# A conditioned residual block with paged attention: condition weights selected on chip, second tile transposed by TensorE, three transfers moved to other places in their queues

## The chip, the cores and the metric

The kernel runs on one core of a Trainium2 chip. The core has TensorE (PE, matmuls; PEld is its weight load), VectorE (DVE), ScalarE (ACT), GpSimd (POOL) and the sync engine (SP), which here only issues DMAs. The metric is the device time of one launch in microseconds (us). Times are given as the median of several runs; one further execution was recorded by the profiler and is what all rows are taken from.

## The reference

The input x has 64 sequences (B) of 32 tokens (S) with 512 features (HID), float32. Two layers are added to it in turn.

```python
# layer 0: every sequence has a condition 0..15; its 32x32 matrix mixes the tokens
x = x + einsum('bct,bcd->bdt', x, weights[condition])
# layer 1: attention over a paged cache, 32 query heads, 8 key heads, D = 128
q, k, v = x @ Wq.T, x @ Wk.T, x @ Wv.T          # 4096, 1024, 1024 wide
q, k = rope(rmsnorm(q) * q_norm_w, pos), rope(rmsnorm(k) * k_norm_w, pos)
# cached keys and values: 16 pages of 32 rows per sequence, by block table
scores = q @ concat(k_cache[table], k).T / sqrt(128), cached rows >= cache_seqlens masked
x = x + softmax(scores) @ concat(v_cache[table], v) @ Wo.T
```

`pos` is the sequence's cache length plus the token's number. The block table and the lengths are inputs, so pages are addressed from registers or by indirect DMA.

## The kernel before

**Tiles and steps.** A tile is 4 sequences x 32 tokens = 128 rows, so there are 16 tiles (NT). The heads are done in two halves (hh = 0, 1) of 4 key heads and 16 query heads; a step is one tile of one half, 32 steps in all. The second half reads back what the first left in DRAM: the partial output `acc_d` (`x1_a`, L344) and the transposed mixed input `x1t_d` (`x1_t`, L350).

**A step.** The tile's input is mixed by a block-diagonal 128x128 matrix `bd`, which holds four condition matrices (`x1_c`, L356: one matmul, one addition on DVE), and transposed by PE (`x1_b`, L363; ACT copies it to `x1t` and stores it). Then come projections of 512 columns each, four accumulating matmuls: one for k, one for v and four for q (`project`, L401). k and q pass through `norm_rope` (L409): a square on ACT, a mean and five passes on DVE, a power on POOL. Their result has tokens in the partitions and has to be turned, so that the head dimension lies there. In the first tile PE does that (`to_columns`, L483: four transposes per projection, two copies by ACT). In all other tiles DVE transposes blocks of 32x32 into `rows` (`turn_rows`, L451), and 16 DMAs of 80 KB from SP move the blocks across partitions into `q_cols` (batches 0 to 2) and `q_last` (batch 3) (`spread`, L463). `by_tensor` (L473) chooses.

**A batch** is one sequence of a step. SP loads its 16 key pages of 64 KB (`load_k`, L280; two buffers `k_t`, so the pages of the batch after next wait until the present one's keys are copied out), DVE copies each head's keys to `kh` (`head_keys`), PE computes the scores of the cached keys (`ps`), ACT their exponential (`pr`), PE the values (`po`), DVE the normalisation. Cached values come by indirect DMA from POOL (`fetch`, L311, rows in `v_row`), and ACT masks them into place (`fill`, L328). The new tokens' scores are made once per step (`new_scores`, `psn`, L584) and their values after that (`new_values`, `pnv`, L601). The output projection of the step before stands in slots 8 and 9 (`pout`, L512).

**Order.** A step has 16 slots (4 batches x 4 key heads). The loop from L909 writes the order out by hand, slot by slot; `pieces` (L866) says which parts of the next tile's preparation go into which slot. PE and SP execute in exactly that order (`manual_schedule`, L88); DVE, ACT and POOL do so in the opening, and are ordered by the scheduler after it. Each engine and each DMA queue runs in order, so one that waits holds up all that stands behind it.

**The opening** (L765 to L864) is written by hand for the first tile and part of the second. SP issues the input and the first query weight, then the 16 pages of the first batch, then the query weight 2, the value weight, the second tile's input, the query weight 3. POOL gathers the first tile's condition matrices row by row (`w_sel`, L771, by an index made on DVE in L726), then issues the key weight, query weight 1, and the page table and lengths for all batches (`pages_at`, `lens_at`). From those DVE makes `v_row` and the masks (`cached_rows`, L160). Filler matmuls (`keep_warm`, L787) run on PE in between. The second tile's k and v projections stand in the opening, its q projections in slots 4 to 7.

**Weights of the second half** are brought in parts near the change of halves: those of k, q, v by SP in steps 14 and 15, the eight parts of the output weights (each two DMAs of 256 KB) by POOL in steps 16 and 17 (`second_outputs`, L908).

Of the kernel before, what the change touches and what calls it, by code (L numbers as in the profile page):

```python
# [11 lines left out]
F32 = mybir.dt.float32  # L12
I32 = mybir.dt.int32
AF = mybir.ActivationFunctionType
ALU = mybir.AluOpType
AX = mybir.AxisListType
# [33 lines left out]
WARM = 16  # L50
# [5 lines left out]
def cond_resid_paged_attention_kernel(  # L56
# [130 lines left out]
    def steps_of(exact, pools):  # L187
# [46 lines left out]
        def load_w(kind, hh, g=0, part=slice(0, 4), eng=nc.sync):  # L234
# [11 lines left out]
            if kind == "o" and not exact:  # L246
                src = src.rearrange("(h j p) e -> h p j e", h=REP, p=S)
                for h in range(part.start, part.stop):
                    eng.dma_start(t[h * S : (h + 1) * S, :, :], src[h])
                return  # L250
            eng.dma_start(t[:, part, :], src.rearrange("(c p) e -> p c e", p=P)[:, part, :])

        def load_parts(which, hh, at, eng=nc.sync):

            if 0 <= at < 2 * len(which):
                kind, g = which[at // 2]
                load_w(kind, hh, g, slice(at % 2 * 2, at % 2 * 2 + 2), eng)
# [22 lines left out]
        def load_k(hh, b):  # L280
# [12 lines left out]
            for j in range(NPP):  # L293
# [12 lines left out]
            last_k[:] = [ins.ins]  # L306
            return k_raw
# [165 lines left out]
        def by_tensor(st):  # L473
            return st.n == 0 or exact
# [8 lines left out]
        def to_columns(st, i):  # L483

            pt = transposed(rows[:, :, i, :], f"{i}_{st.name}")
            p4 = pt.rearrange("p h (b s) -> p b h s", b=BT)
            n = BT - 1
            nc.scalar.copy(q_cols[:, :, i, :].rearrange("p b (h s) -> p b h s", h=4), p4[:, 0:n])  # L488
            nc.scalar.copy(
                columns(st, n)[:, i, :].rearrange("p (h s) -> p h s", h=4), p4[:, n]  # L490
            )
# [48 lines left out]
        class Batch:  # L540


            def __init__(self, st, bt):
                self.st, self.bt = st, bt
                self.n = st.n * BT + bt
                self.name = f"{st.name}_{bt}"
                self.b = st.t * BT + bt
                self.k_raw = load_k(st.hh, self.b)
                self.k, self.pr = {}, {}
                self.v_t = v_bufs[self.b % 2]  # L550
# [173 lines left out]
        if not exact:  # L724
            nc.scalar.dma_start(cond_0, cond[:, 0:1])
            nc.vector.tensor_scalar(cond_0, cond_0, float(S), row, ALU.mult, ALU.add)  # L726
# [3 lines left out]
        if exact:  # L730
# [34 lines left out]
        first, second = steps[0:2]  # L765
        x1_a(first)
        load_w("q", 0, 0)
        nc.scalar.dma_start(lens_sb, lens)
        nc.scalar.dma_start(freq, inv_freq.partition_broadcast(P))
        w_sel = work.tile([P, S], F32, tag="o", name="w_sel", bufs=1)  # L770
        nc.gpsimd.indirect_dma_start(  # L771
            out=w_sel,
            out_offset=None,
            in_=w_cond,
            in_offset=bass.IndirectOffsetOnAxis(ap=cond_0, axis=0),
        )
        nc.scalar.dma_start(cond_row, cond.rearrange("(i s) t -> s t i", s=S)[0:1])
        load_w("k", 0, eng=nc.gpsimd)
        load_w("q", 0, 1, eng=nc.gpsimd)
        batch = Batch(first, 0)  # L780
        load_w("q", 0, 2)
# [3 lines left out]
        later = Batch(first, 1)  # L785

# [10 lines left out]
        positions()  # L797
        trig = work.tile([P, 3, TRIG * HD], F32, tag="w1", name="trig0", bufs=1)
        angles(0, trig)
# [3 lines left out]
        x1_c(first)  # L803
        keep_warm(6)
# [46 lines left out]
        v_a(second)  # L851
# [14 lines left out]
        def pieces(st):  # L866
            do = {
# [10 lines left out]
            if st is second:  # L878
                do[2] = do[3] = do[13] = ()
            return do  # L880
# [27 lines left out]
        second_outputs = [(0, 10), (0, 13), (0, 15), (1, 1), (1, 3), (1, 4), (1, 5), (1, 6)]  # L908
        for st in steps:  # L909
# [3 lines left out]
            for bt in range(0 if st.n else 1, BT):  # L913
                this, after = batch, None
                n = st.n * BT + bt + 2
                if n < NHH * NT * BT:
                    after = Batch(steps[n // BT], n % BT)
                    unfilled += [(after, c) for c in range(VC)]
                for g in range(GH):
# [35 lines left out]
                    if slot == 13 and beyond:  # L955
                        x1_t(beyond)
# [8 lines left out]
                    if (st.n - NT, slot) in second_outputs:  # L965
                        at = second_outputs.index((st.n - NT, slot))
                        load_parts(outputs, 1, at, nc.gpsimd)
# [95 lines left out]
```

## Time and profile before

| what | us |
|---|---|
| median of 3 runs (lowest, highest) | 2183.66 (2181.93, 2184.26) |
| the profiled execution's own time | 2188.01 |
| its span, first to last instruction | 2186.2 |
| PE busy | 2150.5 |
| DVE busy | 1199.1 |
| ACT busy | 866.9 |
| POOL busy | 813.1 |

The granted clock of TensorE is 0.995 on average. In a row of the order in time, "x8" counts instructions that were merged into it, and the bracket gives the engine's idle time before it and what ended it. A float32 matmul is recorded as two instructions, so a projection of four is "x8".

### The profile page before, as it was taken

What the parts mean: (1) busy time and instruction counts of PE and PEld (TensorE: products, weight loads), DVE (VectorE), ACT (ScalarE), POOL (GpSimd) and SP (SyncE); (2) the same over time, 40 slices, a digit from 0 to 9 for tenths busy, and PEclk for the clock granted to TensorE, in tenths of its full rate; (3) what the DMA queues carried; (4) which work ended last, traced back from release to release, by engine and by line L of the source; (5) the groups of instructions that cost most, each with busy time, mean ns of one, the idle gap of its engine ahead of it and who ended that gap; (6) DMA issues with size and microseconds to landing.
All of it is one profiled execution on the core that took longest, in us unless ns stands there. A gap on an engine that the chain in (4) does not pass through costs nothing.

```text
span 2186.2 us, 41553 instructions
## 1 busy us (share of the span) xinstructions
PE 2150.5 (98%) x12970; PEld 1498.3 (69%) x12970; DVE 1199.1 (55%) x2881; ACT 866.9 (40%) x1574; POOL 813.1 (37%) x1024
## 2 busy tenths in 40 slices
PE   8889999999999999999999999999999999999998
PEld 5657776677766677766776667777667777667775
DVE  5655556665465554555554556545556445556442
ACT  3434444444333444333433334443334433334441
POOL 4433333343333433343334434333334333334330
PEclk9999999999999999999999999999999999999999
DMA  8665555556555555556767655555555555555651
GB/s 245 172 166 161 169 159 150 153 159 171 157 152 142 167 161 165 158 146 195 237 176 198 174 154 165 167 163 163 149 158 162 170 163 160 149 160 158 175 159 57
DMA packets 386839, 358.78 MB, mean 164 GB/s; under 512 B 54736, under 2 KB 316896, under 8 KB 386608
## 3 DMA queue, kind: packets, MB, share of 16 engines
q1 hardware_dynamic: 340608, 210.90, 34.3%
q0 software_dynamic: 42992, 140.86, 22.6%
q10 hardware_dynamic: 3008, 4.25, 0.5%
q8 instruction: 106, 1.74, 0.3%
q14 instruction: 125, 1.02, 0.2%
HBM read 302.59 MB, written 12.58 MB: 144 GB/s over the span
## 4 chain that ended last, share of the span: by engine, by line
PE 95%; DMA 2%; issue 1%; DVE 1%; ACT 0%; SPq 0%; POOL 0%; ACTq 0%; DVEq 0%; POOLq 0%
PE po_x L631 21%; PE ps_x L573 20%; PE pout_x L519 20%; PE pp_q_x L404 19%; PE pp_k_x L404 5%; PE pp_v_x L404 5%; PE pnv_x L615 2%; PE psn_x L591 1%; DMA raw_x<-in_vc_dram,v_row 1%; PE pmix_x L360 1%; DMA pages_at<-in_pages_v_dram 0%; DMA x1t_x<-x1t_d 0%; DMA k_t_x<-in_kt_dram 0%; PE px1t_x L368 0%; SPq L468 0%
## 5 line engine op out<-in xcount | busy, mean ns | idle before, releaser
L318 POOL DMA_INDIRECT raw_x<-in_vc_dram,v_row x512 | 538.2, 1051 | 828.3 <-ACT v_x L331 756.2
L581 ACT ACTIVATE pr_x<-ps_x 128x512 f32<-128x512 f32 x512 | 305.7, 597 | 818.2 <-PE ps_x L573 757.3
L631 PEld LDWEIGHTS po_x<-v_x,pr_x 128*128 128x128 f32 x4096 | 516.1, 192 | 129.8 <-issue 115.4
L631 PE MATMUL po_x<-v_x,pr_x 128*128 128x129 f32 x4096 | 551.6, 278 | 4.9 <-ACT v_x L331 1.9
L404 PE MATMUL pp_q_x<-wq_x,x1t_x 128*128 128x512 f32 x1024 | 462.5, 594 | 3.4 <-ACT kh_x L564 3.4
L519 PE MATMUL pout_x<-wo_x,ot_x 128*128 128x512 f32 x1024 | 450.2, 592 | 0.0
L573 PE MATMUL ps_x<-q_cols_x,kh_x 128*128 128x128 f32 x3072 | 405.7, 275 | 0.5 <-ACT q_cols_x L488 0.2
L573 PEld LDWEIGHTS ps_x<-q_cols_x,kh_x 128*128 128x128 f32 x3072 | 376.3, 192 | 17.1 <-issue 16.6
L331 ACT ACTIVATE v_x<-raw_x,valid 128x512 f32<-128x512 f32 x512 | 363.2, 716 | 16.5 <-DMA raw_x<-in_vc_dram,v_row 16.5
L519 PEld LDWEIGHTS pout_x<-wo_x,ot_x 128*128 128x128 f32 x1024 | 189.7, 190 | 214.3 <-issue 214.3
L404 PEld LDWEIGHTS pp_q_x<-wq_x,x1t_x 128*128 128x128 f32 x1024 | 185.4, 191 | 188.8 <-issue 185.2
L566 DVE COPY kh_x<-k_t_x 128x512 f32<-128x512 f32 x506 | 206.1, 417 | 191.8 <-PE ps_x L573 162.0
L649 DVE TENSOR_TENSOR nv_x<-po_x,nv_x 128x258 f32<-128x258 f32 x256 | 108.3, 423 | 317.7 <-PE po_x L631 282.5
L421 POOL TENSOR_TENSOR rs_q_x<-ms_q_x,minus_half 128x4 f32<-128x4 f32 x128 | 140.2, 1096 | 175.9 <-DVE ms_q_x L419 174.8
L414 ACT ACTIVATE sq_q_x<-pp_q_x 128x512 f32<-128x512 f32 x128 | 76.4, 597 | 271.9 <-PE pp_q_x L404 165.3
L573 PE MATMUL ps_x<-q_last_x,kh_x 128*128 128x128 f32 x1024 | 135.2, 275 | 2.9 <-DVE kh_x L566 2.9
L527 DVE TENSOR_TENSOR acc_x<-pout_x,acc_x 128x512 f32<-128x512 f32 x32 | 22.1, 692 | 199.5 <-PE pout_x L519 199.5
L573 PEld LDWEIGHTS ps_x<-q_last_x,kh_x 128*128 128x128 f32 x1024 | 124.6, 192 | 3.1 <-issue 3.1
L404 PE MATMUL pp_k_x<-wk_x,x1t_x 128*128 128x512 f32 x256 | 118.1, 605 | 2.8 <-DMA x1t_x<-x1t_d 2.5
L418 DVE TENSOR_REDUCE ms_q_x<-sq_q_x 128x4 f32<-128x512 f32 x128 | 86.4, 675 | 53.2 <-ACT sq_q_x L414 51.2
L404 PE MATMUL pp_v_x<-wv_x,x1t_x 128*128 128x512 f32 x256 | 115.2, 592 | 0.0
L652 DVE TENSOR_TENSOR o_x<-nv_x,rden 128x256 f32<-128x256 f32 x256 | 108.5, 424 | 6.5
(106 smaller groups left out, 1472.3 us busy)
## 6 DMA issues: line engine op xcount, KB each, us to landing
k_t_x<-in_kt_dram SPq DMA_DIRECT2D x2048, 64.0 KB
q_cols_x<-rows_x SPq DMA_DIRECT2D x372, 80.0 KB
q_last_x<-rows_x SPq DMA_DIRECT2D x124, 80.0 KB
raw_x<-in_vc_dram,v_row POOLq DMA_INDIRECT x512
acc_x<-in_x_dram SPq DMA_DIRECT2D x16, 256.0 KB
x1t_d<-x1t_x ACTq DMA_DIRECT2D x16, 256.0 KB
wo_x<-in_wo_dram SPq DMA_DIRECT2D x16, 256.0 KB
acc_d<-acc_x SPq DMA_DIRECT2D x16, 256.0 KB
```

The lines of the kernel that those rows point to most:

```text
L318: nc.gpsimd.indirect_dma_start(out=raw.rearrange("p g d -> p (g d)"), out_offset=None, in_=vc, in_offset=bass.IndirectOffsetOnAxis(ap=v_ro ...
L331: nc.scalar.activation(v_bufs[b % 2][:, c, :, 0:D], raw, AF.Copy, scale=ok)
L404: nc.tensor.matmul(pp, st.x1t[:, c, :], w[:, c, :], start=(c == 0), stop=(c == KC - 1))
L418: nc.vector.tensor_reduce(ms, sq, AX.X, ALU.add)
L421: nc.gpsimd.tensor_tensor(rs, ms, minus_half, ALU.pow)
L519: nc.tensor.matmul(st.po, st.ot[:, i, :], wt["o", st.hh, i // 4][:, i % 4, :], start=(i == 0), stop=(i == QH - 1),)
L566: last["dve"] = nc.vector.tensor_copy(k, ba.k_raw[:, :, g, :]).ins
L573: nc.tensor.matmul(ps[:, c, :], ba.k[g][:, c * P : (c + 1) * P], queries(ba, g), start=True, stop=True,)
L581: last["act"] = nc.scalar.activation(pr, ps, AF.Exp, scale=SCALE).ins
L631: nc.tensor.matmul(ba.po[:, g % 2, :], ba.pr[g][:, c, :], ba.v_t[:, c, g, :], start=(c == 0), stop=(c == VC - 1),)
L649: nc.vector.tensor_tensor(t, ba.po, t, ALU.add)
L652: nc.vector.tensor_tensor(ba.o[:, both, :], t[:, :, 0:D], rd.unsqueeze(2).to_broadcast([P, 2, D]), ALU.mult,)
```

## The change

- **Condition weights.** The gather and its index are gone. SP loads all 16 matrices (64 KB) into the first 32 partitions, right behind the first tile's input; three copies put them into the other partition groups; DVE compares each row's condition with the numbers 0 to 15 (from an iota on POOL), multiplies and sums, and fills `bd`. The mixing `x1_c(first)` now stands ahead of `positions` and the first `angles`. The first filler is 10 matmuls rather than 16.
- **Third query weight.** `load_w("q", 0, 2)` goes from SP, behind the first batch's pages, to POOL's queue, behind query weight 1 and ahead of `pages_at` and `lens_at`.
- **Second tile.** `by_tensor` holds for it too: no DVE transposes of blocks and no spread. `to_columns` takes the engine of its copies: ACT for k, DVE for the four q; they stand in slots 12 to 14 of the first step. `v_a(second)` moves from the opening to slot 13.
- **Input read back.** A step's last batch issues only the first eight of its sixteen pages; the others follow in slot 13, after `x1_t`.
- **Output weights of the second half.** SP issues them, and in other slots: part 0 in step 16, parts 1 to 7 in step 17.

```diff
-WARM = 16
+WARM = 10
...
             if kind == "o" and not exact:
                 src = src.rearrange("(h j p) e -> h p j e", h=REP, p=S)
                 for h in range(part.start, part.stop):
-                    eng.dma_start(t[h * S : (h + 1) * S, :, :], src[h])
+                    nc.sync.dma_start(t[h * S : (h + 1) * S, :, :], src[h])
...
-        def load_k(hh, b):
+        def load_k(hh, b, first_pages):
...
-            for j in range(NPP):
+            def load_page(j):
                 ins = nc.sync.dma_start(
...
-            last_k[:] = [ins.ins]
-            return k_raw
+                last_k[:] = [ins.ins]
+
+            for j in range(first_pages):
+                load_page(j)
+            return k_raw, [lambda j=j: load_page(j) for j in range(first_pages, NPP)]
...
         def by_tensor(st):
-            return st.n == 0 or exact
+            return st.n < 2 or exact
...
-        def to_columns(st, i):
+        def to_columns(st, i, copy=nc.scalar.copy):
...
-            nc.scalar.copy(q_cols[:, :, i, :].rearrange("p b (h s) -> p b h s", h=4), p4[:, 0:n])
-            nc.scalar.copy(
-                columns(st, n)[:, i, :].rearrange("p (h s) -> p h s", h=4), p4[:, n]
-            )
+            copy(q_cols[:, :, i, :].rearrange("p b (h s) -> p b h s", h=4), p4[:, 0:n])
+            copy(columns(st, n)[:, i, :].rearrange("p (h s) -> p h s", h=4), p4[:, n])
...
             nc.scalar.dma_start(cond_0, cond[:, 0:1])
-            nc.vector.tensor_scalar(cond_0, cond_0, float(S), row, ALU.mult, ALU.add)
...
+        number_i = small.tile([P, NCOND], I32, tag="number_i", name="number_i", bufs=1)
+        nc.gpsimd.iota(number_i, pattern=[[1, NCOND]], base=0, channel_multiplier=0)
         x1_a(first)
+        w_all = work.tile([P, NCOND, S], F32, tag="pr", name="w_all", bufs=3)
+        nc.sync.dma_start(w_all[0:S], w_cond.rearrange("(n s) e -> s n e", s=S))
         load_w("q", 0, 0)
...
-        w_sel = work.tile([P, S], F32, tag="o", name="w_sel", bufs=1)
-        nc.gpsimd.indirect_dma_start(
-            out=w_sel,
-            out_offset=None,
-            in_=w_cond,
-            in_offset=bass.IndirectOffsetOnAxis(ap=cond_0, axis=0),
-        )
...
         load_w("k", 0, eng=nc.gpsimd)
         load_w("q", 0, 1, eng=nc.gpsimd)
+        load_w("q", 0, 2, eng=nc.gpsimd)
         batch = Batch(first, 0)
-        load_w("q", 0, 2)
         load_w("v", 0)
...
-        positions()
-        trig = work.tile([P, 3, TRIG * HD], F32, tag="w1", name="trig0", bufs=1)
-        angles(0, trig)
+
+        for i, copy in enumerate((nc.vector.tensor_copy, nc.scalar.copy, nc.vector.tensor_copy), 1):
+            copy(w_all[i * S : (i + 1) * S], w_all[0:S])
+        own = small.tile([P, NCOND], F32, tag="own", name="own", bufs=1)
+        nc.vector.tensor_copy(cond_f, cond_0)
+        nc.vector.tensor_scalar(own, number, cond_f, None, ALU.is_equal)
+        nc.vector.tensor_tensor(
+            w_all, w_all, own.unsqueeze(2).to_broadcast([P, NCOND, S]), ALU.mult
+        )
+        w_sel = work.tile([P, S], F32, tag="o", name="w_sel", bufs=1)
+        nc.vector.tensor_reduce(w_sel, w_all.rearrange("p n e -> p e n"), AX.X, ALU.add)
         for i in range(BT):
             blk = slice(i * S, (i + 1) * S)
             nc.vector.tensor_copy(bd[blk, blk], w_sel[blk, :])
         x1_c(first)
+        positions()
+        trig = work.tile([P, 3, TRIG * HD], F32, tag="w1", name="trig0", bufs=1)
+        angles(0, trig)
         keep_warm(6)
...
-        v_a(second)
...
         def pieces(st):
...
+            if st is second:
+                by_vector = nc.vector.tensor_copy
+                return {
+                    4: (lambda st: q_a(st, 0),),
...
+                    12: (lambda st: to_columns(st, GH), lambda st: to_columns(st, 0, by_vector)),
+                    13: (v_a, lambda st: to_columns(st, 1, by_vector)),
+                    14: (
+                        lambda st: to_columns(st, 2, by_vector),
+                        lambda st: to_columns(st, 3, by_vector),
+                    ),
+                }
...
-        second_outputs = [(0, 10), (0, 13), (0, 15), (1, 1), (1, 3), (1, 4), (1, 5), (1, 6)]
+        second_outputs = {
+            (0, 10): (0,),
+            (1, 2): (1,),
+            (1, 4): (2,),
+            (1, 5): (3, 4),
+            (1, 6): (5, 6),
+            (1, 7): (7,),
+        }
...
-                    after = Batch(steps[n // BT], n % BT)
+                    after = Batch(steps[n // BT], n % BT, NPP // 2 if bt == BT - 1 else NPP)
...
-                    if slot == 13 and beyond:
-                        x1_t(beyond)
+                    if slot == 13:
+                        if beyond:
+                            x1_t(beyond)
+                        for load in after.pages_left if after else ():
+                            load()
...
-                        load_parts(outputs, 1, at, nc.gpsimd)
+                        load_parts(outputs, 1, at)
```

## The prediction

> **What bounds the kernel now.** I read the page's busy times first, then the waits of TensorE (PE), then the order in time around each wait.
>
> ```profile
> PE 2150.5 (98%) x12970; PEld 1498.3 (69%) x12970; DVE 1199.1 (55%) x2881; ACT 866.9 (40%) x1574; POOL 813.1 (37%) x1024
> ...
> PE psn_x L591 <- DMA q_cols_x<-rows_x: 7.7, 1, 7.7
> PE pp_q_x L404 <- ACT kh_x L564: 3.4, 1, 3.4
> PE ps_x L573 <- DVE kh_x L566: 2.9, 1, 2.9
> PE pp_k_x L404 <- DMA x1t_x<-x1t_d: 2.5, 1, 2.5
> PE po_x L631 <- ACT v_x L331: 1.9, 2, 1.3
> ```
>
> PE is busy 98% of the span, so only its waits (us in total, times, longest) and slow stretches can be shortened. By the order in time nearly all fall before 119 us; from there PE is busy throughout (the windows 120 to 1000 and 1500 to 2100 us show no idle time), but for one wait at 1066, one at 1198 and the tail. What the change can win lies in the opening and in those two. The lines that carry them (start us, us, engine line, what; in brackets the idle time before and its releaser):
>
> ```profile
> 7.01 8.96 DMA pages_at<-in_pages_v_dram
> ...
> 16.06 0.35 DVE L164 TENSOR_SCALAR v_row<-pages_at,row 128x256 int32<-128x256 int32 x1 [2.88 <-DMA pages_at<-in_pages_v_dram]
> ...
> 22.48 0.39 SPq L251 DMA_DIRECT2D wq_x<-in_wq_dram  x1
> ...
> 29.86 5.37 PE L404 MATMUL pp_q_x<-wq_x,x1t_x 128*128 128x512 f32 x8 [3.37 <-ACT kh_x L564]
> ...
> 94.62 0.70 DVE L454 STREAM_TRANSPOSE rows_x<-rope_q_x 128x512 f32<-128x512 f32 x1
> ...
> 97.23 6.51 SPq L468 DMA_DIRECT2D q_cols_x<-rows_x  x8
> 110.22 2.41 SPq L468 DMA_DIRECT2D q_last_x<-rows_x  x4
> ...
> 116.72 0.60 PE L591 MATMUL psn_x<-q_cols_x 128*32 128x128 f32 x2 [7.74 <-DMA q_cols_x<-rows_x]
> ...
> 1193.25 0.37 SPq L354 DMA_DIRECT2D x1t_x<-x1t_d  x1
> ...
> 1200.99 5.37 PE L404 MATMUL pp_k_x<-wk_x,x1t_x 128*128 128x512 f32 x8 [2.45 <-DMA x1t_x<-x1t_d]
> ```
>
> The reader is to see: PE stood at 26.5 for the third query weight, which SP issued at 22.48 behind 16 key pages (the ACT copy named as releaser was only the last other event); it stood 7.74 us for the second tile's spread, four of whose DMAs left SP at 110.22; and at 1198 for the projection input, issued behind a batch's 16 pages.
>
> **1. The condition weights (L771, L802).** Out goes a gather that POOL issues in 1.04 us; bd was complete at 10.20. In comes a 64 KB load right behind the input's on SP, three copies between partition groups (two on VectorE (DVE), one on ACT), a compare, a multiply, a reduce, and the same four copies to bd. The load's landing isn't in this trace. Bounds: not before the condition column (chain: 0.74 + 3.12 = 3.86), not after the weight issued behind it was in (about 7); I take 4.7, as it is nearer to the first in size. Then DVE: 2 x 0.42 (as kh copies 128x512), about 0.25 for the small two, 0.69 (as L361), 0.69 (as L418), 0.79 for bd: 3.3 us, bd at 8.0, 2.2 us sooner. PE adds 1.87 (pmix), DVE 0.69: mixed input at 10.6 instead of 12.85. But positions and the first angles now follow that addition on DVE: 0.4 + 2.1 us (7.09 to 9.16 before), then ACT's sine, abs and cosine (9.19 to 10.13 before: 0.94), and on ACT these stand ahead of the x1t copy (14.85 before). 10.6 + 0.4 + 2.1 + 0.94 gives 14.0: the copy gains 0.8 at best and loses 2.2 if the load lands at 7. Neither moves the end: what the first projections feed, DVE's chain from 16.06, waits for pages_at. Value: 0. WARM 16 to 10 only shortens filler in that wait.
>
> **2. Third query weight on POOL's queue (L782).** It is issued before pages_at and lens_at, which wait behind it on that queue. Its 1.05 MB at the 295 GB/s of the window 10 to 20 us take 3.6 us; on the other side POOL is free of the gather (1.04) and of its wait for the condition (1.04), so wk leaves 2.0 us sooner. pages_at lands S later: bounds 0 (the sooner start used in full and transfers closer packed) and 3.6 (start useless); I take 1.5. Behind pages_at stand, in DVE's order, the row numbers, four masks, the second angles and the norms of q0, k, q1, q2, each 3.6 us (21.51, 25.12, 28.74). The fourth started at 35.95, because its matmul ended at 35.23; freed of the weight it follows the third at 32.4 + S. ACT's squares, key copies and exponentials hang on that. Gain 3.55 - S = 2.1 (0 to 3.5). SP, one DMA lighter, issues wv at about 22.5, and wv is needed at 33.
>
> [...] The row: the DMA engines were 89% and 93% busy from 10 to 30 us. [...] I keep S = 1.5.
>
> **3. Second tile by TensorE, values projection in slot 13.** Removed: 16 spread DMAs on SP (0.59 each), five DVE transposes (0.71 each), the wait of 7.74 and the slow work after it: psn took 2.12 (1.01 in the next step), the po after it 1.60 (1.06): 1.65. Added on PE: 20 transposes, 0.44 per four (46.84 to 47.28): 2.2. Added copies: two on ACT (0.47, 0.28), eight on DVE, where PSUM reads of 128x258 take 0.43: some 2.8 us, at slots 12 to 14, with DVE idle 3.3 and 12 us just after. The last copies have 4.9 us of PE work ahead of new_scores to hide in (pmix 0.86, px1t 0.44, four groups of 0.9); without that cover they would cost about 1.5. Sure part: 7.74 + 1.65 - 2.2 = 7.2.
>
> v_a (3.44 us of PE at 52.98) leaves the opening for slot 13. The new_scores, fills, gathers and the query norms then start 3.4 us sooner, and DVE (busy 9.8 of 10 us at 80 to 90) loses 0.63 us net per query. Four PE waits in 74 to 102 hang on these: 0.59, 1.45, 2.90, 1.34, together 6.3. I take 4.0 back (0 to 6.3): PE gets to them sooner too, and gathers compete with wo loads (a gather issued at 65.74 landed at 74.0). Key pages of the following batches, freed from the spread on SP, aren't late.
>
> **4. Input read back sooner, outputs on SP.** With eight pages deferred, x1t's load leaves 8 x 0.54 = 4.3 us sooner and no output weights of POOL's queue contend. The two waits go: 2.45 and 0.39. Also pp_k at 1200.99 took 5.37 instead of 3.60: 1.77. [...] The row says 4.6: the granted clock was 0.68 in 1201 to 1206.4. (After the 2.90 us at 94.6 it stayed 1.00, so the wait's length doesn't settle it.) I take the row. Cost: 14 wo DMAs go to SP in step 17; 12 stand ahead of the third batch's pages and take 12 x 0.47 = 5.6, and SP was idle there from 1215.7 to 1225.2. Their 3 MB may delay gathers: 0.3 (0 to 1.5). Value 4.3. In the 14 steps without the wait nothing changes, nor in the first half of the steps, where the deferred pages follow the others at once.
>
> **Sum.** 0 + 2.1 + 7.2 + 4.0 + 4.3 = 17.6 us of the profiled span of 2186.2: 2168.6. That execution took 2188.01, 4.35 above the median shown; on the median 2183.66 - 17.6 = 2166.
>
> **Rivals.**
> *Waits re-form (0.24).* Part 3's 4.0 doesn't come, because PE runs into the gathers and keys 10 us sooner while the DMA engines are 98% busy at 70 to 80; only what is removed by hand counts: 17.6 - 4.0 - 1.5 for new waits = 12, time 2172. For it: every one of those waits is behind DVE, ACT or a gather; against it: SP stood idle 103.7 to 110.2.
> *pages_at late (0.12).* S = 3.6 or more: part 2 gives 0 or a little less, 15 in all, 2169.
> *All clears (0.08).* 3.5 + 7.2 + 6.3 + 4.6: 21.6, 2162.
> *Slower (0.04).* x1t has one buffer, so its load waits on SP for v_a of the same slot, in 16 steps, and now eight key pages stand behind it. A delay w in each lets key copies come w later; against 17.6 it decides at 1.1 us of PE wait per step. Against it: at 1317.59 eight pages are out at 1321.9, v_a ended at 1320.2, and the three key copies that waited until 1331.3 end at 1332.4, 5.6 before their scores at 1338.0. Were w 6.9, 1.3 us a step would be paid, 20.8 in all: 2187.
> *The change doesn't do what it says (within the first case):* the selection on chip brings the first projection nothing, as worked out in 1.
>
> **How the numbers follow.** Forecast 0.52, the rivals 0.48. No change means within 0.2%, 4.4 us, about what a measurement tells apart. All cases but one are faster by more: 0.95; same 0.01; slower 0.04. Range: 2161 is the forecast with the upper ends of parts 2 and 3; 2175 is the re-formed waits with S = 3.6 and a gather wait in step 17. It leaves out some 0.15.
>
> **What would show it.** No wait of psn near 105 us; the third query projection directly after the first transposes, at full clock or not, at 26 to 29; v_row at 16 to 19.6; the x1t copy within 1 us of 14.8; no wait at pp_k in steps 14 and 17; PE busy 98.5% or more. Wrong: a PE wait over 3 us between 60 and 110, waits in each step after 940, or DVE's v_row past 20.

## The result, and the profile after

The changed kernel takes 2170.47 us (median of five runs, 2169.88 to 2172.92). The kernel before, run beside it, takes 2182.78 us (2181.93 to 2184.26). The ratio is 0.9946, with a 95% interval of 0.9932 to 0.9960: 12.3 us faster, where 17.6 were forecast (2166). It lies inside the range of 2161 to 2175, and above the forecast by 4.5 us. The profiled execution of the changed kernel took 2170.36 us, 0.1 below its median; its span is 2168.5.

The busy times on the page of the changed kernel:

```profile
PE 2144.9 (99%) x12978; PEld 1495.3 (69%) x12978; DVE 1200.4 (55%) x2890; ACT 865.2 (40%) x1578; POOL 806.8 (37%) x1009
```

Its waits of TensorE (us in total, times, longest):

```profile
PE pt_x L451 <- DVE rows_x L443: 6.5, 1, 6.5
PE pmix_x L363 <- DVE bd L811: 2.7, 1, 2.7
PE warm L791 <- POOL ident masks.py:199: 1.6, 1, 1.6
PE ps_x L574 <- ACT q_cols_x L491: 1.5, 3, 0.6
PE pp_q_x L407 <- ACT x1t_x L373: 1.1, 1, 1.1
PE pnv_x L616 <- ACT nv_x L624: 1.0, 1, 1.0
```

The waits of the spread (7.7), of the third query weight (3.4), of the key copies (2.9) and of the projection input (2.5) are all gone. Parts 3 and 4 took their waits away. But the list is headed by a wait that is new: 6.5 us in which TensorE stood for the first normalized query. In the order in time it looks like this:

```profile
5.76 0.58 POOL L795 DMA_DIRECT2D pages_at<-in_pages_v_dram  x1
...
22.14 2.20 ACTq L271 DMA_DIRECT2D bd<-in_w_cond_dram  x4
22.48 0.35 DVE L164 TENSOR_SCALAR v_row<-pages_at,row 128x256 int32<-128x256 int32 x1 [8.15 <-DMA pages_at<-in_pages_v_dram]
...
26.52 0.31 ACT L150 ACTIVATE sin<-trig 128x128 f32<-128x128 f32 x1 [11.54 <-DVE trig L149]
...
27.98 0.69 DVE L421 TENSOR_REDUCE ms_q_x<-sq_q_x 128x4 f32<-128x512 f32 x1 [1.49 <-ACT sq_q_x L417]
...
32.12 1.12 PE L451 MATMUL pt_x<-ident,rows_x 128*128 128x128 f32 x4 [6.51 <-DVE rows_x L443]
...
33.02 5.08 PE L407 MATMUL pp_q_x<-wq_x,x1t_x 128*128 128x512 f32 x8
```

VectorE stood 8.15 us for pages_at and began the row numbers at 22.48, against 16.06 before: S is 6.4 us, where the prediction took 1.5 and allowed 0 to 3.6. All behind it on VectorE moved along: the first norm, in the kernel before

```profile
21.51 0.69 DVE L418 TENSOR_REDUCE ms_q_x<-sq_q_x 128x4 f32<-128x512 f32 x1 [1.49 <-ACT cos L152]
```

now starts at 27.98, and the third query projection at 33.02 instead of 29.86. The opening lost 3.2 us there, where 2.1 should have been gained.

The same comparison along the whole span. A step ends where the next step's new_scores (psn) begin; a step without waits takes 67.13 us, and 65.83 in the second half of the steps. Lengths in us:

| stretch | before | after | gained |
|---|---|---|---|
| opening, to the first new_scores | 57.40 | 58.11 | -0.71 |
| first step (after: with the second tile's values projection, 3.44) | 51.18 | 49.67 | 1.51 |
| second step | 76.81 | 67.13 | 9.68 |
| the two steps with a wait for the projection input | 66.46 and 70.22 | 65.83 and 65.83 | 5.02 |
| last step and end | 70.10 | 68.94 | 1.16 |
| the other steps together | | | 1.06 |
| span | 2186.24 | 2168.52 | 17.72 |

So the profiled span fell by 17.7 us, almost to the tenth what the sum forecast, by terms that are not those of the sum.

### The profile page after: what moved, and what is told of

It is laid out like the page before. It is cut to its first block, busy times and chain, and to the rows that moved or that the text cites. A ratio compares the mean times of both kernels' runs of the same rounds, so it can differ in the third digit from the quotient of the medians.

```text
span 2168.5 us, 41562 instructions
## 1 busy us (share of the span) xinstructions
PE 2144.9 (99%) x12978; PEld 1495.3 (69%) x12978; DVE 1200.4 (55%) x2890; ACT 865.2 (40%) x1578; POOL 806.8 (37%) x1009
## 4 chain that ended last, share of the span: by engine, by line
PE 97%; DMA 1%; DVE 1%; ACT 0%; issue 0%; POOL 0%; POOLq 0%; DVEq 0%; ACTq 0%
PE po_x L632 22%; PE ps_x L574 21%; PE pout_x L520 20%; PE pp_q_x L407 20%; PE pp_v_x L407 5%; PE pp_k_x L407 5%; PE pnv_x L616 2%; PE psn_x L592 1%; DMA pages_at<-in_pages_v_dram 1%; PE pmix_x L363 1%; PE px1t_x L371 0%; PE pt_x L451 0%; ACT sq_q_x L417 0%; ACT q_cols_x L491 0%; POOL wq_x L251 0%
## 5 line engine op out<-in xcount | busy, mean ns | idle before, releaser
L574 PEld LDWEIGHTS ps_x<-q_cols_x,kh_x 128*128 128x128 f32 x3072 | 376.2, 192 | 17.8 <-issue 14.8
```

The source lines that it names most:

```text
L574: nc.tensor.matmul(ps[:, c, :], ba.k[g][:, c * P : (c + 1) * P], queries(ba, g), start=True, stop=True,)
```

## The experiments: the opening

Each ratio is to the kernel before on the same chip. The kernel before took 2182.2 to 2186.4 us on the chips of these runs, so medians of different rows are compared by their ratios. "First new_scores" is the length of the opening in the kernel's one profile. It can differ by 1.5 us between profiles of the same opening: in the run with half of part 4 (below), whose opening is that of the kernel before, it is 58.92 instead of 57.40, 1.05 of it because the third query projection ran longer (in the kernel before it takes 5.37 us, 3.41 of them at a granted clock of 0.5). The start of v_row repeats better: 16.06, 15.81 and 15.95 in the three profiles with the opening loads of the kernel before.

| kernel | median, us | ratio to before (95%) | row numbers (v_row) start | first new_scores | span |
|---|---|---|---|---|---|
| before | 2182.78 | 1 | 16.06 | 57.40 | 2186.2 |
| changed | 2170.47 | 0.9946 (0.9932 to 0.9960) | 22.48 | 58.11 | 2168.5 |
| before, part 2 alone | 2184.43 | 1.0001 (0.9991 to 1.0010) | 19.17 | 56.93 | 2185.1 |
| changed, part 1 undone | 2166.89 | 0.9924 (0.9908 to 0.9939) | 18.92 | 54.12 | 2164.5 |
| changed, part 2 undone | 2170.82 | 0.9935 (0.9920 to 0.9951) | 19.27 | 57.66 | 2169.7 |
| changed, pages_at first | 2171.56 | 0.9943 (0.9927 to 0.9959) | 14.88 | 57.83 | 2170.7 |
| ... and bd loads on GpSimd | 2168.98 | 0.9925 (0.9909 to 0.9940) | 13.95 | 51.16 | 2165.4 |
| ... and norm weights behind the key weight | 2163.70 | 0.9911 (0.9896 to 0.9926) | 15.86 | 51.61 | 2161.7 |
| changed, condition weights behind the query weight | 2172.98 | 0.9944 (0.9928 to 0.9960) | 22.45 | 58.29 | 2171.5 |
| changed, norm weights behind the key weight | 2170.01 | 0.9941 (0.9926 to 0.9956) | 20.79 | 56.41 | 2167.0 |
| changed, part 1 undone, pages_at first, bd loads on GpSimd | 2165.21 | 0.9905 (0.9888 to 0.9921) | 13.64 | 50.18 | 2163.5 |

**Part 2 alone, and each of parts 1 and 2 undone.** The theory at first was that the small load's place behind the third weight explains all of S; the rival, that there are two causes.

```diff
# before, with part 2 alone (and the reverse in the changed kernel: part 2 undone)
+        load_w("q", 0, 2, eng=nc.gpsimd)
         batch = Batch(first, 0)
-        load_w("q", 0, 2)
```

> The kernel before with part 2 alone: the third query weight issued on GpSimd's queue ahead of pages_at. As predicted (S = 1.5): pages_at at 17.5, 2.1 us faster. Theory A (6.4 us from the place alone): pages_at at 22.4, 2.9 us slower, near 2185.5. Theory C (3.5 us from the place, the rest from part 1): pages_at at 19.5, the gain of 3.55 us at the fourth projection used up, time within 1 us of before.

> The changed kernel with the third query weight back on SP's queue, behind the first batch's key pages: part 2 alone undone. Theory A (place in the queue behind the third weight explains all of the 6.4 us by which pages_at was late): pages_at lands at 16 as before, the norms at 21.5, but the third query projection waits for the weight as before, near 29.9 to 30.5; 2167 to 2168. Theory C (two causes: the third weight's 3.5 us, and 2.75 us because the first query weight, behind the condition weights on SP, ran into GpSimd's loads of the norm weights, and the key weight with it): pages_at lands near 18.9, the first norm at 24.3, the third query projection at 31 to 33; 2169 to 2171, no difference from the changed kernel that is certain.

```diff
# changed, with part 1 undone
-        w_all = work.tile([P, NCOND, S], F32, tag="pr", name="w_all", bufs=3)
-        nc.sync.dma_start(w_all[0:S], w_cond.rearrange("(n s) e -> s n e", s=S))
         load_w("q", 0, 0)
...
+        w_sel = work.tile([P, S], F32, tag="o", name="w_sel", bufs=1)
+        nc.gpsimd.indirect_dma_start(out=w_sel, out_offset=None, in_=w_cond,
+            in_offset=bass.IndirectOffsetOnAxis(ap=cond_0, axis=0))
         nc.scalar.dma_start(cond_row, cond.rearrange("(i s) t -> s t i", s=S)[0:1])
```

> The changed kernel with part 1 alone undone: the condition weights gathered by GpSimd again, no load of all of them on SP, positions and first angles ahead of the mix, 16 filler matmuls. Theory A (the place behind the third weight explains all of the 6.4 us): pages_at lands at 22.4 or later, for the gather is back ahead of it; time 2170 to 2172. Theory C (two causes): the first query weight lands at 6.8 again instead of 9.6, the key weight at 12.4 instead of 15.1, pages_at at 19.5, the first norm at 25; the opening gains 2.7 us and the time is 2167 to 2168.5. If the condition weights bring more elsewhere than I worked out, the time is above 2172.

The row numbers in these three, in the order in time of each; first before with part 2 alone:

```profile
19.17 0.35 DVE L164 TENSOR_SCALAR v_row<-pages_at,row 128x256 int32<-128x256 int32 x1 [6.80 <-DMA pages_at<-in_pages_v_dram]
```

The changed kernel with part 2 undone, in which TensorE then also stands for the third query weight:

```profile
19.27 0.35 DVE L164 TENSOR_SCALAR v_row<-pages_at,row 128x256 int32<-128x256 int32 x1 [5.74 <-DMA pages_at<-in_pages_v_dram]
...
31.30 6.75 PE L407 MATMUL pp_q_x<-wq_x,x1t_x 128*128 128x512 f32 x8 [1.27 <-DMA wq_x<-in_wq_dram]
```

The changed kernel with part 1 undone:

```profile
18.92 0.35 DVE L164 TENSOR_SCALAR v_row<-pages_at,row 128x256 int32<-128x256 int32 x1 [6.37 <-DMA pages_at<-in_pages_v_dram]
```

Part 2 alone costs S = 19.17 - 16.06 = 3.1 us, part 1 without part 2 19.27 - 16.06 = 3.2, both together 6.4: two causes of equal size that add. With part 2 alone the gain is 3.55 - 3.1 = 0.45 us by the prediction's formula; the opening became 0.47 shorter, which is less than it varies by, and the time did not move measurably. Part 1 is the surprise: it was valued at 0, and undoing it shortens the opening and the span by 4.0 us (the intervals of the two ratios still overlap a little). Undoing part 2 gains nothing certain, because the third weight is then late itself.

**pages_at ahead of the weights.** If the small load's place were the whole of it, moving it up should give back all.

```diff
+        pages_at = work.tile([P, B * VC], I32, tag="pr", name="pages_at", bufs=3)
+        nc.gpsimd.dma_start(pages_at, pages_v)
+        lens_at = work.tile([P, B], I32, tag="pr", name="lens_at", bufs=3)
+        nc.gpsimd.dma_start(lens_at, lens_row.partition_broadcast(P))
         load_w("k", 0, eng=nc.gpsimd)
```

> The changed kernel, with the loads of pages_at and lens_at issued by GpSimd ahead of the key weight and the two query weights instead of behind them. In the changed kernel pages_at landed at 22.4 us (15.96 before), the first norm began at 27.98 (21.51) and the third query projection at 33.02 (29.86). Theory A (place in the queue: the small load stands behind the third weight, and all of VectorE's chain behind it): pages_at lands by 13, the first norm begins near 20.5, when the first projection and the tables are ready, the third query projection near 27 to 28; the opening gains 5 us and the time is 2164 to 2167. Theory B (the weight's bytes, wherever the small load stands): the weights land as in the changed kernel or 0.5 us later, the projections stay within 1 us of where they were, and the time is 2169 to 2171.

It gave nothing: v_row came 7.6 us sooner, the first norm at 27.70, a mere 0.28 sooner, and the third query projection at 32.75. Its first step even took 51.84 us instead of 49.67, because a wait came in that the changed kernel doesn't have (more on it under part 3):

```profile
94.56 1.13 PE L574 MATMUL ps_x<-q_last_x,kh_x 128*128 128x128 f32 x8 [2.02 <-DVE kh_x L567]
```

In the opening a second gate stood right behind the first. ACT in this kernel:

```profile
22.42 3.77 ACTq L271 DMA_DIRECT2D bd<-in_w_cond_dram  x4
26.24 0.31 ACT L150 ACTIVATE sin<-trig 128x128 f32<-128x128 f32 x1 [10.75 <-DMA bd<-in_w_cond_dram]
...
27.09 0.58 ACT L417 ACTIVATE sq_q_x<-pp_q_x 128x512 f32<-128x512 f32 x1
```

Four loads of 4 KB, the second tile's condition weights, are issued by ACT ahead of the second sine and of the squares that every norm begins with. They were not issued before 22.42 and took until 26.2, and all of ACT's work waited behind them. What they waited for stands in the trace's semaphore records. In them each of the four loads waits for the very semaphore that it counts up when it lands, and the load that last used that semaphore is a key page's, issued by SP. Three of those pages had just landed, at 22.40, 24.56 and 25.85; the issues followed at 22.42, 24.58 and 25.87. In the changed kernel it is the same: pages landed at 22.12 and 23.02, and the issues that wait for their semaphores followed at 22.14 and 23.04. So ACT stood here not for data of its own but for another queue's loads, through a shared semaphore. An edit tried another place:

```diff
-        load_cond_weights(1, nc.scalar, mybir.EngineType.Activation)
+        load_cond_weights(1, nc.gpsimd, mybir.EngineType.Pool)
```

> The changed kernel with pages_at and lens_at ahead of the weights on GpSimd's queue, and the four loads of the second tile's condition weights (bd) issued by GpSimd instead of ACT. With pages_at first alone, v_row came at 14.88 but the first norm still at 27.70: ACT issued the four bd loads from 22.42 to 26.2, and the second sine and the squares stood behind them. Theory F (ACT's issue of the bd loads is the second gate, because it waits for key pages that land late): the second sine comes near 19, the first norm near 20, the third query projection at 26 to 28, when the third weight (22.75) is long there; 2164 to 2166. Rival (the DMA engines gate whatever is issued, the keys next): the norms come early but the first scores still wait for key pages, which left SP until 25 to 27; 2168 to 2171.

ACT in this kernel:

```profile
18.14 0.31 ACT L150 ACTIVATE sin<-trig 128x128 f32<-128x128 f32 x1 [3.57 <-DVE trig L148]
...
18.99 0.58 ACT L417 ACTIVATE sq_q_x<-pp_q_x 128x512 f32<-128x512 f32 x1
```

The sine comes at 18.14, the first norm at 19.60, the third query projection at 25.65, the first new_scores at 51.16: the opening is 7 us shorter than in the changed kernel, and theory F holds. The span fell by less, 3.1 us: this run has waits of 1.15 us at 1306 and of 1.2 us in all at 2110, and a last step of 70.5 us instead of 68.9, in places that the edit doesn't touch. The median of 2168.98 is above the 2164 to 2166 that I expected, and by its interval it can't be told from the changed kernel.

**What part 1 does to the queue.** Nothing in part 1 touches GpSimd's queue but the gather that it removes and an iota of 0.18 us. Yet the first query weight, now behind the condition weights on SP, landed at 12.0 instead of 6.8 (the expectations put it at 9.6, which is too early), and the key weight on GpSimd's queue at 15.1 instead of 12.4, although issued 2 us sooner. The packets in the trace show something odd at that time: the first sixteen 4 KB packets of GpSimd's queue took 0.6 to 3.1 us each (0.6 to 1.6 in the kernel before), and most other 4 KB packets 0.16. Sixteen is what one of the two loads of the norm weights has, which stand first on that queue and spread one row of 512 bytes over 128 partitions; the trace doesn't name a packet's load, so I take the sixteen to be theirs. In the kernel before, the query weight's last packets move between 6.0 and 6.3 us, just as those sixteen begin (5.9); in the changed kernel the sixteen begin at 4.7, and the weight's packets move until 11.5. My guess from these times was that slow packets hold up a query weight that is still under way when they begin; how they would do so no trace shows. Two edits try this: the condition weights behind the query weight, or the norm weights out of the way.

```diff
# condition weights behind the query weight
-        nc.sync.dma_start(w_all[0:S], w_cond.rearrange("(n s) e -> s n e", s=S))
         load_w("q", 0, 0)
+        nc.sync.dma_start(w_all[0:S], w_cond.rearrange("(n s) e -> s n e", s=S))
# norm weights behind the key weight (they leave the head of the queue)
         load_w("k", 0, eng=nc.gpsimd)
+        nc.gpsimd.dma_start(norm_w["q"], qn_w.partition_broadcast(P))
+        nc.gpsimd.dma_start(norm_w["k"], kn_w.partition_broadcast(P))
```

> The changed kernel with the load of all condition weights issued by SP behind the first query weight instead of ahead of it. Part 1 alone made pages_at 3.2 us later. Theory G (the condition weights ahead of the query weight push it into the time in which GpSimd's loads of the norm weights, with packets of 600 ns and more, hold the DMA engines): the query weight lands at 6.9 instead of 9.6, the key weight at 12.4 instead of 15.1, pages_at near 19.5; the bd blocks are complete near 11, the x1t copy is at 16 to 17; 2167.5 to 2170. Rival H (GpSimd's queue starts 1.5 us sooner without the gather in it, and it is this that meets the query weight): the query weight still lands at 8.5 or later, the key weight at 14.5 or later, and the time is 2170 to 2173.

> The changed kernel with GpSimd's two loads of the norm weights, which spread one row over 128 partitions, issued behind the key weight instead of ahead of it. Theory J (part 1's 3 us in the transfers come from these loads: their packets of 4 KB took 1.0 to 3.1 us each in the changed kernel, where other packets of that size take 0.16, and the condition weights pushed the first query weight in among them): the first query weight lands by 7.5 instead of 9.6, the key weight near 11.5 instead of 15.1, pages_at at 19.5 instead of 22.4, the first norm at 24.8; the first new_scores start near 55 instead of 58.1, and the time is 3 us below the changed kernel's, a ratio of 0.993 to before. Rival K (the condition weights' 512 small packets skew the DMA engines by themselves): the key weight still lands near 15, pages_at at 22 or later, no gain, a ratio of 0.9945.

The first fell: now the query weight was clear of the slow packets (SP's 2 KB packets ended by 6.5 us), but pages_at still landed at 21.6, and the condition weights met the slow packets instead: the first copy of them could start only at 12.38, the bd blocks were complete at 16.3 and the input's transpose was copied at 22.50. Theory G, as I put it, is wrong. Rival H's reason, that GpSimd's queue starts sooner without the gather, fell too: its first 4 KB packet moved at 6.24, later than in the kernel before (5.91). The second edit gave about half: key weight at 12.9, pages_at at 20.7, v_row and the first new_scores 1.7 us sooner, where theory J said 3; the first query weight landed at 10.2 and not by 7.5. But the move also lets the key weight leave 1.1 us sooner (2.36 instead of 3.49), so it isn't separated whether the slow packets or that start gave the 1.7. So the place of the norm weights accounts for some half of part 1's cost; the other 1.5 us stay open. In medians the 1.7 us can't be told from nothing.

One pattern in the traces narrows it. The key weight's load counts up its semaphore sixteen times in them as its parts land. The counts run from 11.42 to 12.39 in the kernel before and from 11.67 to 15.14 in the changed kernel: the first part is hardly later, the last 2.75 us. In all eight profiles with part 1 the first and last count lie 2.2 to 3.9 us apart, in all six without it 0.9 to 1.0, and the two edits above still have 3.7 and 2.6. So part 1 makes the parts of a load land unevenly, as rival K has it (whose forecast of no gain was wrong), and neither of the two edits removes that. What causes it stays open.

The profile has the time from issue to landing of these loads, in the changed kernel (KB each, us):

```profile
pages_at<-in_pages_v_dram POOLq DMA_DIRECT2D x1, 128.0 KB, 16.6
...
norm_q<-in_qn_w_dram POOLq DMA_DIRECT2D x1, 64.0 KB, 7.1
norm_k<-in_kn_w_dram POOLq DMA_DIRECT2D x1, 64.0 KB, 9.3
```

64 KB take 7 to 9 us, and pages_at 16.6. With part 1 undone:

```profile
wk_x<-in_wk_dram POOLq DMA_DIRECT2D x1, 1024.0 KB, 6.8
pages_at<-in_pages_v_dram POOLq DMA_DIRECT2D x1, 128.0 KB, 11.2
```

and with the norm weights behind it the key weight took 10.5 us.

**Together.** Two kernels collect what the runs point to, one with part 1 undone and one with it kept.

```diff
# part 1 undone, pages_at first, bd loads on GpSimd: the three diffs above together
# part 1 kept: pages_at first, bd loads on GpSimd, norm weights behind the key weight
```

> The changed kernel with part 1 undone (gather by GpSimd, angles ahead of the mix, 16 filler matmuls), pages_at and lens_at ahead of the weights on GpSimd's queue, and the bd loads of the second tile issued by GpSimd. With part 1 undone alone the time was 2166.9, the first norm at 24.37 behind pages_at at 18.82. If place in the queues is what the opening pays for: pages_at by 11, first norm near 20.3, the first projection being at 15.6, the third query projection near 26; 2162 to 2165. If the keys or the weights are then next: 2165.5 to 2167.

> All that the earlier runs point to, with part 1 kept: pages_at and lens_at first on GpSimd's queue, then the key weight, the norm weights, the two query weights; the bd loads of the second tile issued by GpSimd. With pages_at first and the bd loads moved the first new_scores started at 51.16, with part 1 undone as well at 50.18. If theory J holds the key weight and the keys behind it come 2 to 3 us sooner and the start is at 48.5 to 50, a ratio of 0.990 to before; by rival K nothing is gained by it and the start is at 51 or later, 0.991 to 0.9925.

Both beat both kernels: their intervals end at 0.9921 and 0.9926, below the 0.9932 at which the changed kernel's begins. With part 1 kept, in the order in time:

```profile
15.86 0.51 DVE L164 TENSOR_SCALAR v_row<-pages_at,row 128x256 int32<-128x256 int32 x1
...
20.02 0.31 ACT L150 ACTIVATE sin<-trig 128x128 f32<-128x128 f32 x1 [4.86 <-DVE trig L149]
...
21.48 0.69 DVE L421 TENSOR_REDUCE ms_q_x<-sq_q_x 128x4 f32<-128x512 f32 x1 [1.49 <-ACT sq_q_x L417]
...
26.11 3.60 PE L407 MATMUL pp_q_x<-wq_x,x1t_x 128*128 128x512 f32 x8
```

The third query projection comes 6.9 us sooner than in the changed kernel, and at full speed (3.60 instead of 5.08). Its opening is no shorter than without the move of the norm weights (51.61 against 51.16), which is the rival's number: their place gains nothing here that can be seen, and VectorE now waits 0.87 us for them at 15.4. Its span, 2161.7, is the shortest of all, 6.8 below the changed kernel's; by ratio, 0.9911 against 0.9905, the two kernels can't be told apart.

## The experiments: parts 3 and 4

**Part 3 alone, and its values projection put back.**

> The kernel before with part 3 alone: second tile transposed by TensorE, its copies and the values projection in slots 12 to 14. By the prediction's sum 11.2 us (7.2 sure, 4.0 of 6.3 in waits): the third step's new_scores start at 174.2 instead of 185.4, ratio 0.9949. If all of the waits go, 13.5 us: 171.9, ratio 0.9938. If the waits re-form because TensorE runs into gathers and keys sooner: 7.2, a start at 178, ratio 0.9967.

```diff
# changed, with the values projection of the second tile back in the opening
         q_b(first, 3)
+        v_a(second)
         scores(batch, 3)
...
-                    13: (v_a, lambda st: to_columns(st, 1, by_vector)),
+                    13: (lambda st: to_columns(st, 1, by_vector),),
```

> The changed kernel with the second tile's values projection back in the opening, where the kernel before has it; the transposes by TensorE stay. The first new_scores then start 3.44 us later in any case, and slot 13 is 3.44 us shorter. Theory V (moving it out cleared waits of TensorE between 60 and 105 us, as I put it in the prediction): some of the four waits return, 2 us or more together, and the second step's new_scores start at 110 or later instead of 107.8; the ratio to before is 0.9955 or more. Theory W (the spread and its DVE transposes were what those waits hung on): no wait of more than 0.7 us between 62 and 105 us, the third step's new_scores start within 0.5 us of 174.9, the ratio is 0.994 to 0.995.

Part 3 alone: ratio 0.9953 (0.9937 to 0.9969), the third step's new_scores at 173.85 instead of 185.38. That is 11.5 us, where the sum had 11.2. But TensorE had no wait of over 0.3 us between 61 and 1054 us, so all four waits went, 6.3 us and not 4.0; the profile of this run has a half-speed stretch at 62 us (granted clock 0.72 in 62 to 68), which took 1.6 back (below). Two lines of its waits show that part 4's wait is there undisturbed:

```profile
PE pp_q_x L404 <- DMA wq_x<-in_wq_dram: 4.1, 1, 4.1
PE pp_k_x L404 <- DMA x1t_x<-x1t_d: 4.1, 2, 2.9
```

With the projection back in the opening, all waits of TensorE:

```profile
PE pt_x L451 <- DVE rows_x L443: 6.7, 1, 6.7
PE pmix_x L363 <- DVE bd L811: 2.5, 1, 2.5
PE warm L791 <- POOL ident masks.py:199: 1.6, 1, 1.6
PE pnv_x L616 <- ACT nv_x L624: 1.0, 1, 1.0
PE pp_q_x L407 <- ACT x1t_x L373: 0.7, 1, 0.7
PE ps_x L574 <- ACT q_cols_x L491: 0.5, 2, 0.3
```

None of the four came back, so theory V falls: they did not hang on the projection. Theory W holds for the waits, not for its start of the third step: that is 175.8, 0.9 later than the 174.9 that it gave; this profile has the half-speed stretch too (0.93 in 62 to 68 us, 0.79 in 68 to 74). This run doesn't separate the spread from VectorE's transposes. For the longest of the four, the 2.90 us for key copies, another one says more: with pages_at first, and without the spread and its transposes, the wait of 2.02 us at 94.6 is of the same kind, and VectorE was busy without a gap up to those copies. So I take that wait to hang on VectorE's backlog, of which the five transposes were a part; it can come back. Moving the projection was worth nothing that can be measured: ratio 0.9949 (0.9934 to 0.9965) against 0.9946. The projection costs 2.3 us in the opening instead of its 3.44 (first new_scores at 60.43 instead of 58.11), since it covers waits of 1.1 us there.

**Half of part 4.**

```diff
-                    after = Batch(steps[n // BT], n % BT)
+                    after = Batch(steps[n // BT], n % BT, NPP // 2 if bt == BT - 1 else NPP)
...
+                        for load in after.pages_left if after else ():
+                            load()
# the output weights stay where the kernel before has them
```

> The kernel before with one half of part 4: eight key pages of each step's last batch issued behind the projection input's load; the output weights stay on GpSimd's queue. The step with the wait took 70.22 us in the profile of before, against 65.83 for a step without waits. Theory D (the load is late because it stands behind 16 pages): it leaves 4.3 us sooner, the wait of 2.45 us and the slow matmuls after it go, that step takes 65.9 and the time falls by 4 to 5 us, to 2178 to 2180. Rival E (the output weights on GpSimd's queue hold it up): at least 1.5 us of wait stays, and less than 3 us are gained.

The time is 2181.66, ratio 0.9980 (0.9971 to 0.9989), some 4.4 us below the kernel before on that chip. In the order in time at the same place:

```profile
1188.12 0.33 SPq L357 DMA_DIRECT2D x1t_x<-x1t_d  x1
...
1198.71 3.60 PE L407 MATMUL pp_k_x<-wk_x,x1t_x 128*128 128x512 f32 x8
1202.91 1.43 DVE L569 COPY kh_x<-k_t_x 128x512 f32<-128x512 f32 x4 [5.48 <-DMA k_t_x<-in_kt_dram]
1203.39 1.16 PE L576 MATMUL ps_x<-q_cols_x,kh_x 128*128 128x128 f32 x8 [1.08 <-DVE kh_x L569]
```

The projection no longer waits, at full speed (3.60): theory D holds for its wait. But that step took 67.18 us, not 65.9: the key pages, now behind the input, came late themselves, and TensorE stood 1.08 us for the copy of them. In the changed kernel, in which the output weights also left GpSimd's queue, the step takes 65.83. So the order of issue is worth some 3.0 of the 4.4 us in that step. The rest I put down to the output weights by elimination; moving them alone was not run, and as this step took 69.0 to 71.6 us in three profiles with the order of before, the split is good to 1 us or so. Where the wait only changes its object, as it did here, a run of one half shows what the other half is for.

## Why the prediction was right, and where it was wrong

The median lies in the range, and parts 3 and 4 were right in their mechanism. Parts 1 and 2 were not, and two of the signs that the prediction had set came out against it: v_row started at 22.48, past the 20 that was to show it wrong, and the third query projection at 33.02, not at 26 to 29.

*Part 1, "Neither moves the end" and "Value: 0": this step failed.* The selection itself went as worked out: bd complete at 8.4 (8.0 forecast), the x1t copy at 14.41 (within 1 us of 14.8). What was left out is the lateness of other loads once it is there: the first query weight on its queue landed at 12.0 us instead of 6.8, the key weight on GpSimd's at 15.1 instead of 12.4, and pages_at was 3.2 later. Costed were the instructions added and the landing of the load, not the lateness that it passes on. Its size is 3.2 us of S, and 4.0 us of the opening; how it comes about is known for about half of it at most.

*Part 2, S:* alone it measured 3.1, inside the bounds of 0 to 3.6; I took 1.5. The bound of 3.6, the weight's 1.05 MB at the 295 GB/s of 10 to 20 us, was nearer than my choice: in the kernel before, SP issued that weight at 22.48, but the 14 us before it (8.40 to 22.45) were no unused room, since the DMA engines were 89% busy from 10 to 20 us and 93% from 20 to 30. With part 1 the bounds broke, at 6.4, because they were worked out for part 2 alone. The rival "pages_at late" is what came, and by more than I had put into it.

*Part 3:* the sure 7.2 held, and all 6.3 us of the waits went, not 4.0. With the projection at its measured 2.3 us, the first two steps gained 1.51 + 9.68 + 2.3 = 13.5 us, which is 7.2 + 6.3. The reason for it was half wrong: the projection's move clears nothing. The rival "waits re-form" didn't come in the changed kernel; in the one with pages_at first 2.0 us of it did.

*Part 4:* 4.3 forecast, 5.0 found in the two steps. The row (4.6, with the slow matmuls at a granted clock of 0.68), and not the two waits alone (2.45 + 0.39 = 2.8), was right to take.

*The sum:* 17.6 forecast for the profiled span, 17.7 found, by cancellation. Parts 1 and 2 gave -3.0 (opening -0.71, less the 2.3 us by which the moved projection had relieved it; an opening varies by 1.5) instead of +2.1; part 3 gave 2.3 more than forecast, part 4 0.7 more, and 2.2 us lie in steps and in an end that the change doesn't touch. So the hit is luck in part: what parts 1 and 2 missed by, 5.1 us, was made good by errors the other way. The lower end of the range is a slip besides: with the upper ends of parts 2 and 3 the forecast is 2162.3, not 2161.

*The median:* a step failed here too: "on the median 2183.66 - 17.6". The sum was taken from the waits of an execution that stood 5.2 us above its median of 2182.78, and subtracted from the median. The changed kernel's profiled execution stood within 0.1 us of its own median, so in medians 12.3 are left of 17.7. The 2.2 us outside the change are of a kind that varies: the last step took 67.07 to 71.07 us over all profiles. So does the wait for the input: the step with it took 70.22, 71.56 and 69.01 us in three profiles with that part of the kernel before. How the 5.2 us are spread over runs without a profile stays open.

## What to carry to other kernels

When a load is put ahead of others, follow the lateness to the smallest load at the end, on other queues too, and cost two such edits together, not each against the old profile: here a load put ahead on SP's queue cost 3.2 us on GpSimd's, and 3.1 and 3.2 us became 6.4 on one small table behind which all of VectorE stood. When a gate is removed and nothing moves, look which engine is blocked right behind it: here four loads of 4 KB issued by ACT held all of its arithmetic until 26.2 us, three of them until a key page of SP's queue with the same semaphore had landed. And before a sum of waits is taken off a median, take off what the profiled execution itself was above that median.

## What the runs showed of the hardware

In some of these kernels a load that spreads one row over 128 partitions from GpSimd's queue was slow out of proportion. The first sixteen 4 KB packets of that queue, which I take for a norm weight's, took 0.6 to 3.1 us in the changed kernel where most others take 0.16, and in the kernel with pages_at first thirteen of the sixteen 2 KB packets of the lens_at load took 1.1 to 1.8 us, between 7.7 and 11.8 us. The spread alone doesn't do it: in the changed kernel the same lens_at load, moved between 17.7 and 22, took 0.08 to 0.12 us a packet. What makes the difference stays open. The load of freq, spread in the same way but from ACT's queue, moved in packets of 256 bytes that took 0.018 us.

In the changed kernel the eight loads that GpSimd issued before 7 us landed in the order of their issue, the last part of each at 7.04, 9.36, 12.18, 15.14, 18.45, 21.92, 22.39 and 22.59 us.

A wait of 0.95 us ahead of the second pnv (54 to 65 us) is in all fourteen profiles. In four of them the granted clock fell to half for 3.41 us, 1.6 to 2.3 us after the wait ended; in ten it didn't, with the same matmuls around it. The window 62 to 68 us, with the granted clock behind the five engines; first the changed kernel, then the one with part 2 undone:

```profile
62.00:68.00 6.00, 5.05 (x31) 3.49 (x31) 1.73 (x5) 4.74 (x12) 1.24 (x2) 1.00 0.36 100
```

```profile
62.00:68.00 6.00, 5.46 (x28) 3.78 (x29) 1.73 (x5) 4.35 (x12) 1.69 (x2) 0.73 0.40 102
```

It costs 1.7 us of the step (51.35 against 49.67), which is as much as some of the edits tried here, and only profiles tell it from them.
